# Two output stores split into 120 and 8 rows, so that fifteen and eight DMA engines carry them instead of sixteen

## The chip, the core and the metric

The kernel runs on one core of a Trainium2 chip. The core has computing engines that run side by side, each on its own list of instructions: TensorE (PE; its weight loads are shown as PEld), VectorE (DVE), ScalarE (ACT) and GpSimd (POOL). SyncE (SP) computes nothing here and issues transfers. Transfers between the chip's memory (HBM) and the on-chip memory (SBUF, 128 partitions) are carried by sixteen DMA engines. The results of TensorE land in PSUM and are copied from there to SBUF by VectorE or ScalarE before they can be stored.

The metric is the time of one execution on the device, in microseconds (us), taken without the profiler. The profile comes from an execution of its own, which is longer.

## What is computed

The reference takes 1,024 sequences of 50 item numbers, their lengths, and a table of 100,001 embeddings of 128 numbers. It gathers the embeddings, takes running means, normalises them, runs a spiking recurrence over the 50 steps, and multiplies the spike counts with the whole table. Cut to what matters:

```python
emb = emb_table.at[0].set(0.0)
e = emb[seq]                                   # 1024 x 50 x 128
uF = cumsum(e, axis=1) / minimum(t, lengths)
y = (uF - mean) * rsqrt(var + BN_EPS) * gamma + beta
# 50 steps: v = v + (x - v) / TAU ; spike = v >= V_TH ; v = v - spike * V_TH
uF_out = spikes.mean(axis=0)                   # 1024 x 128
scores = uF_out @ emb.T                        # 1024 x 100001, float32
```

The output has 1,024 x 100,001 x 4 bytes, 409.6 MB. The table is 51.2 MB.

## The kernel before

The first stage is the gather and the recurrence. The second stage, which the change touches, makes the product with the table. The table is worked through in 98 blocks of 1,024 rows (`HALF`), and these in 22 groups `c` of the widths below. For each group, the eight blocks `n` of 128 sequences follow one another. For each `n` an output tile `o` of 128 partitions is filled block by block: matmuls into PSUM (`product`), then a copy with the factor 1/50 into `o`, on VectorE and ScalarE in turn. Then one store sends the whole tile out.

```python
P = 128
HALF = 1024
KQ = HALF // P                                  # 8
WIDTHS = 4 * [2] + 4 * [3] + 11 * [6] + [4, 4, 4]
NARROW, MIDDLE = 4, 8
# ...
    def store(n, c0, o):
        nc.sync.dma_start(out=out[n * P : (n + 1) * P, c0 : c0 + o.shape[1]], in_=o)
```

From group 8 (`MIDDLE`) on, three tiles of six blocks take turns, so the tile of one store is filled again three stores later:

```python
                turns = [(rowp, "rows2", 6), (rowp, "rows3", 6), (op, "o", 6)]
# ...
        for n in range(NB):
            # ...
            pool, tag, most = turns[blocks % len(turns)]
            blocks += 1
            o = pool.tile([P, most * HALF], F32, tag=tag, name=f"o_{c}_{n}")
            for q in range(q0, q1):
                # ... matmuls of block q into po
                if turn % 2 == 0:
                    nc.vector.tensor_scalar_mul(o[:, h0 : h0 + hw], po[:, :hw], 1.0 / T)
                else:
                    nc.scalar.mul(o[:, h0 : h0 + hw], po[:, :hw], 1.0 / T)
                turn += 1
                # ...
            if c or n > 1:
                store(n, q0 * HALF, o[:, : min(N, q1 * HALF) - q0 * HALF])
            # ...
            if n in (1, 4) and c >= MIDDLE and to_fetch < parts:
                # ... ScalarE issues the load of three more blocks of the table
```

Below, store (c,n) is the one of group c and block n. A store of groups 8 to 18 has 128 rows of 6,144 numbers, 24,576 bytes a row. The last three groups have four blocks each, 16,384 bytes a row. The last block of the table has 673 rows; it is loaded in two small transfers, 128 x 5 rows and 33 rows of 512 bytes.

Of the kernel before, what the change touches and what calls it, by code (L numbers as in the profile page):

```python
# [20 lines left out]
P = 128  # L21
BN_EPS = 1e-5
V_TH = 1.0
HALF = 1024
KQ = HALF // P
# [4 lines left out]
HELD = AHEAD * GROUP + LATE  # L30

WIDTHS = 4 * [2] + 4 * [3] + 11 * [6] + [4, 4, 4]
NARROW, MIDDLE = 4, 8


@with_exitstack
def rec_kernel(
# [9 lines left out]
    nc = tc.nc  # L47
    B, T = seq.shape
    N, D = table.shape
# [24 lines left out]
    parts = -(-N // HALF)  # L74
    assert sum(WIDTHS) == parts
    rows = {}
# [6 lines left out]
    def size(q):  # L83
        return min(HALF, N - q * HALF)

    def slot(q):

        if q < GROUP + LATE:
            return 0, q % GROUP
        return (q - LATE) // GROUP, (q - LATE) % GROUP  # L90

    def group(g):
        at = g if g < AHEAD else AHEAD - 2 + g % 2
        r = rowp.tile([P, GROUP, HALF], F32, tag=f"rows{at}", name=f"rows_{g}")
        for k in range(GROUP):
            rows[g * GROUP + k + (LATE if g else 0)] = r[:, k, :]
        return r

    def fetch(r, q, n):

        engine = nc.sync if q < HELD else nc.scalar
        k = slot(q)[1]
        n = min(n, parts - q)
        whole = n - (size(q + n - 1) < HALF)
        if whole:
            engine.dma_start(
                out=r[:, k : k + whole, :],
                in_=table[q * HALF : (q + whole) * HALF, :].rearrange("(q p k) d -> p q (k d)", p=P, k=KQ),
            )
        if whole < n:  # L110
            full, rest = divmod(size(parts - 1), P)
            c1 = (parts - 1) * HALF
            r = r[:, k + whole, :].rearrange("p (k d) -> p k d", d=D)
            if full:
                engine.dma_start(
                    out=r[:, :full, :],
                    in_=table[c1 : c1 + full * P, :].rearrange("(k p) d -> p k d", p=P),
                )
            if rest:
                engine.dma_start(out=r[:rest, full, :], in_=table[c1 + full * P : N, :])  # L120
# [21 lines left out]
    def prepare(q, pt):  # L142
        turned(q, pt)
        split[q] = hi, lo = free.pop(0)
        hw = size(q)
        if hw % 2:
            nc.vector.memset(hi[:, hw : hw + 1].bitcast(F32), 0.0)
            nc.vector.memset(lo[:, hw : hw + 1].bitcast(F32), 0.0)
        vp, vh, vl = views(q, pt, hi, lo)
        nc.scalar.copy(vh, vp)  # L150
        nc.vector.tensor_tensor(vl, vp, vh.bitcast(F32), ALU.subtract)  # L151
# [3 lines left out]
    def product(po, q, n, k0, kw):  # L155
        kw += kw % 2
        for j, part in enumerate(split[q]):
            nc.tensor.matmul(  # L158
                po[:, :kw],
                lhsT=counts[n],  # L160
                rhs=part[:, k0 : k0 + kw],
                start=j == 0,
                stop=j == 1,
            )

    def store(n, c0, o):
        nc.sync.dma_start(out=out[n * P : (n + 1) * P, c0 : c0 + o.shape[1]], in_=o)


    with ExitStack() as ph:  # L170
# [132 lines left out]
        for t in range(T):  # L303
# [10 lines left out]
            pieces = halves if not last else halves[:1] + [slice(B - 3 * P, B), slice(BANK, BANK + P)]  # L314
# [102 lines left out]
        for q, (pool, tag, po) in enumerate(((gp, "e", sums), (up, "uF", [po1[:, cs] for cs in halves]))):  # L417
            o = pool.tile([P, HALF], F32, tag=tag, name=f"o_0_{q}")
            for h, cs in enumerate(halves):
                product(po[h], q, 0, h * BANK, BANK)  # L420
            for h, cs in enumerate(halves):
                if q and h:
                    nc.vector.tensor_scalar_mul(o[:, cs], po[h], 1.0 / T)
                else:
                    nc.scalar.mul(o[:, cs], po[h], 1.0 / T)
                store(0, q * HALF + h * BANK, o[:, cs])
# [10 lines left out]
    q0 = 0  # L437
    to_split = WIDTHS[0]
    to_fetch = HELD

    def places(at):
        t = rowp.tile([P, GROUP, HALF], F32R, tag=f"rows{at}", name=f"pairs_{at}")
        free.extend((t[:, k, :], t[:, k + 1, :]) for k in range(0, GROUP, 2))

    for c, W in enumerate(WIDTHS):

        if c in (0, NARROW, MIDDLE):
            opening.close()
            where = opening if c < MIDDLE else ctx
            op = where.enter_context(tc.tile_pool(name="o", bufs=1, reuse_waits="tile"))  # L450
            if c == 0:
                third = [op.tile([P, HALF], F32R, tag=x, name=x) for x in ("hi2", "lo2")]
                free.append(third)
                turns = [(op, f"o{k}", 2) for k in range(4)]
            elif c == NARROW:
                assert third in free
                free.remove(third)
                turns = [(op, f"o{k}", 3) for k in (2, 0, 1)]
            else:
                fourth = op.tile([P, 4, HALF], F32R, tag="pairs", name="pairs")  # L460
                free.extend((fourth[:, k, :], fourth[:, k + 1, :]) for k in (0, 2))
                turns = [(rowp, "rows2", 6), (rowp, "rows3", 6), (op, "o", 6)]
            blocks = 0
        q1 = q0 + W
        q2 = q1 + (WIDTHS[c + 1] if c + 1 < len(WIDTHS) else 0)

        def ready():
            nonlocal to_split
            if to_split < q2 and free:
                prepare(to_split, psum.tile([P, HALF], F32, tag="ps", name=f"pt_{to_split}"))  # L470
                to_split += 1

                if to_split in (GROUP + LATE, 2 * GROUP + LATE):
                    places(to_split // GROUP - 1)

        for n in range(NB):
            if c == 0 and n == 0:
                continue
# [4 lines that stand above are left out]
                h0 = (q - q0) * HALF  # L483
                hw = size(q)
                po = psum.tile([P, HALF], F32, tag="ps", name=f"po_{n}_{q}")
                for k0 in range(0, hw, BANK):
                    product(po[:, k0 : k0 + BANK], q, n, k0, min(BANK, hw - k0))
# [5 lines that stand above are left out]
                if c == 0 and n == 1:  # L493
                    store(n, q * HALF, o[:, h0 : h0 + hw])
                if n == NB - 1:
                    free.append(split.pop(q))
                    ready()
            if c or n > 1:
                store(n, q0 * HALF, o[:, : min(N, q1 * HALF) - q0 * HALF])
            if 2 <= n < NB - 1:  # L500
                ready()

            if n in (1, 4) and c >= MIDDLE and to_fetch < parts:
                g, k = slot(to_fetch)
                if k or to_split >= (g - 1) * GROUP + LATE:
                    if k == 0:
                        r = group(g)
                    fetch(r, to_fetch, GROUP // 2)
                    to_fetch += GROUP // 2
        assert to_split == q2  # L510
        q0 = q1
# [19 lines left out]
```

## Time and profile before

| | |
|---|---|
| time of one execution, median of 3 | 1574.13 us (1574.05 to 1574.31) |
| the profiled execution | 1643.7 us from the first to the last instruction |
| written to HBM, read from HBM | 409.6 MB, 77.7 MB |
| busy in the span: PE, PEld, DVE, ACT, POOL | 67%, 50%, 58%, 38%, 23% |
| copies PSUM to `o`: VectorE, ScalarE | 391 of 1221 ns each, 391 of 1018 ns each |
| stores of 3,072 KB (six blocks) | 88 |
| loads of 1,536 KB during the second stage | 19 |
| one issue of a store on SyncE | 332 ns |

The page of a profile has six parts: busy times; the span in forty slices, with a digit for the busy share of each engine and of the sixteen DMA engines together; the DMA queues; the chain of work that ended last; the costliest groups of instructions; and the issues of transfers. In the chain, each step is followed back to what released it: "DMA scores<-o" there is the time from the issue of a store to its landing. A line of the waits such as "ACT o L491 <- DMA scores<-o" means that line 491 on ScalarE, which writes a tile `o`, waited for the store of that tile's earlier contents; the numbers after it are the total in us, how often, and the longest.

A store has landed when all the DMA engines that carry it have reported. The trace has these reports one by one, sixteen for a whole store, and a record for each row that was moved, with its start, size and duration.

### The profile page before, as it was taken

The page shows a single profiled execution, that of the slowest core. Times are in us where ns is not written, and L with a number is a line of the kernel's source. Part 1 is how long each engine was busy: PE and PEld are TensorE (multiplying, and loading weights), DVE is VectorE, ACT ScalarE, POOL GpSimd, SP SyncE. Part 2 cuts the span into 40 slices and gives each one's busy share as a digit, 9 for nine tenths or more (in the row PEclk, how much of TensorE's full clock was granted, in tenths as well). Part 3 has the DMA queues.
Part 4 walks back from the last instruction along what each step waited for, and adds up shares of the span by engine and source line. Part 5 has one row for each costly group of instructions (what it writes and reads, how often), then busy time and mean ns, then how long its engine had stood idle before and what let it go on. Part 6 is the DMA issues. An engine that isn't in the chain of part 4 may idle for free.

```text
span 1643.7 us, 12618 instructions
## 1 busy us (share of the span) xinstructions
PE 1108.6 (67%) x4548; PEld 825.2 (50%) x4548; DVE 945.6 (58%) x1165; ACT 630.2 (38%) x700; POOL 378.3 (23%) x406
## 2 busy tenths in 40 slices
PE   4334334344343499888988888878788887887885
PEld 2122122122122276666866666666666666665664
DVE  4566566566575766566655555555545554554553
ACT  2222222222222255455544444444444444443442
POOL 7666666666666500000000000000000000000000
PEclk9975555555555599999999999999999999998998
DMA  9511111111112179999999999999999999999998
GB/s 340 216 46 48 47 46 49 47 45 48 49 45 70 39 319 416 403 422 417 400 427 431 429 429 424 423 424 423 426 427 415 416 419 429 427 408 415 391 424 361
DMA packets 54859, 488.14 MB, mean 297 GB/s; under 512 B 12139, under 2 KB 12940, under 8 KB 32524
## 3 DMA queue, kind: packets, MB, share of 16 engines
q1 hardware_dynamic: 33424, 429.81, 62.3%
q0 software_dynamic: 12800, 26.24, 6.1%
q10 hardware_dynamic: 8572, 31.28, 4.8%
q8 instruction: 36, 0.59, 0.1%
q14 instruction: 27, 0.22, 0.0%
HBM read 77.69 MB, written 409.60 MB: 296 GB/s over the span
## 4 chain that ended last, share of the span: by engine, by line
DMA 47%; DVE 23%; another core or an unknown queue 11%; PE 9%; ACT 6%; issue 3%; DVEq 0%; POOL 0%; ACTq 0%; SPq 0%; POOLq 0%
DMA scores<-o 46%; PE po L158 9%; DVE bs L340 4%; ACT o L491 4%; DVE uF L332 4%; DVE v L377 4%; DVE s L360 3%; DVE negv L295 3%; DVE o L489 2%; DVE a L370 1%; DMA e<-in_L_rec_emb_table,idx 1%; DVE mv L348 1%; DVE q L367 1%; ACT v L374 0%
## 5 line engine op out<-in xcount | busy, mean ns | idle before, releaser
L489 DVE TENSOR_SCALAR o<-po 128x1024 f32<-128x1024 f32 x391 | 464.2, 1221 | 357.5 <-DMA scores<-o 304.1
L491 ACT ACTIVATE o<-po 128x1024 f32<-128x1024 f32 (+1 forms) x391 | 387.6, 1018 | 550.8 <-DMA scores<-o 331.1
L201 POOL DMA_INDIRECT e<-in_L_rec_emb_table,idx x400 | 377.7, 944 | 184.2 <-issue 112.8
L158 PE MATMUL po<-pairs,countB 128*128 128x512 f32 x1136 | 304.2, 414 | 65.9 <-ACT o L491 50.8
L158 PEld LDWEIGHTS po<-pairs,countB 128*128 128x128 f32 x1136 | 218.4, 197 | 129.0 <-ACT o L491 65.7
L158 PE MATMUL po<-pairs,countC 128*128 128x512 f32 x852 | 232.4, 419 | 49.4 <-ACT o L491 49.3
L267 PE MATMUL pre<-zT,l 128*128 128x512 f32 x100 | 74.4, 746 | 251.3 <-DVE uF L332 203.5
L158 PEld LDWEIGHTS po<-pairs,countC 128*128 128x128 f32 x852 | 164.5, 199 | 94.9 <-ACT o L491 61.0
L267 PEld LDWEIGHTS pre<-zT,l 128*128 128x128 f32 x100 | 27.7, 278 | 291.3 <-issue 175.0
L332 DVE SCALAR_TENSOR_TENSOR uF<-rlen,pre 128x512 f32<-128x512 f32 (+1 forms) x101 | 68.1, 674 | 167.5 <-remote 154.8
L352 ACT ACTIVATE r<-mv,eps 128x1 f32<-128x1 f32 x50 | 14.7, 295 | 364.6 <-DVE mv L348 297.8
L151 DVE TENSOR_TENSOR pairs<-pt,pairs 128x1024 fp32r<-128x1024 f32 x71 | 86.3, 1222 | 88.5 <-ACT pairs L150 88.3
L128 PE MATMUL pt<-ident,rows 128*128 128x128 f32 x782 | 110.1, 287 | 9.6 <-ACT o L491 5.7
L128 PEld LDWEIGHTS pt<-ident,rows 128*128 128x128 f32 x782 | 98.7, 150 | 30.8 <-ACT o L491 9.8
L323 PE MATMUL pre<-ident,e 128*128 128x128 f32 x400 | 102.1, 423 | 15.9 <-DMA e<-in_L_rec_emb_table,idx 13.8
L323 PEld LDWEIGHTS pre<-ident,e 128*128 128x128 f32 x400 | 85.7, 224 | 47.7 <-DMA e<-in_L_rec_emb_table,idx 23.9
L278 PE MATMUL sums<-s,ident_h 128*128 128x512 bf16 x98 | 49.6, 609 | 75.4 <-DVE s L360 44.3
L158 PE MATMUL po<-hi,countB 128*128 128x512 f32 x216 | 89.0, 412 | 16.3 <-ACT o L491 11.4
L158 PE MATMUL po<-lo,countB 128*128 128x512 f32 x216 | 86.2, 401 | 0.0
L150 ACT CAST pairs<-pt 128x1024 fp32r<-128x1024 f32 x71 | 71.8, 1012 | 13.7 <-PE pt L128 13.4
L158 PE MATMUL po<-hi,countC 128*128 128x512 f32 (+1 forms) x162 | 67.9, 419 | 13.6 <-ACT o L491 13.6
L158 PE MATMUL po<-pairs,countA 128*128 128x512 f32 x284 | 71.3, 395 | 8.1 <-ACT o L491 8.0
(75 smaller groups left out, 876.4 us busy)
## 6 DMA issues: line engine op xcount, KB each, us to landing
scores<-o SPq DMA_DIRECT2D x88, 3072.0 KB
scores<-o SPq DMA_DIRECT2D x32, 1536.0 KB
scores<-o SPq DMA_DIRECT2D x16, 2048.0 KB
scores<-o SPq DMA_DIRECT2D x30, 1024.0 KB
rows<-in_L_rec_emb_table ACTq DMA_DIRECT2D x19, 1536.0 KB
rows<-in_L_rec_emb_table SPq DMA_DIRECT2D x6, 3072.0 KB
scores<-o SPq DMA_DIRECT2D x8, 1872.5 KB
e<-in_L_rec_emb_table,idx POOLq DMA_INDIRECT x400
```

The costliest lines, as they stand in the source:

```text
L128: nc.tensor.transpose(pt[:, k0 : k0 + kw], r[:kw, k0 : k0 + D], ident[:kw, :kw])
L150: nc.scalar.copy(vh, vp)
L151: nc.vector.tensor_tensor(vl, vp, vh.bitcast(F32), ALU.subtract)
L158: nc.tensor.matmul(po[:, :kw], lhsT=counts[n], rhs=part[:, k0 : k0 + kw], start=j == 0, stop=j == 1,)
L201: nc.gpsimd.indirect_dma_start(out=es[t][:, n * P : (n + 1) * P], out_offset=None, in_=table, in_offset=bass.IndirectOffsetOnAxis(ap=idx[: ...
L267: nc.tensor.matmul(pre[h], lhsT=l, rhs=zT[:, h * BANK : (h + 1) * BANK], start=t == 0, stop=False, skip_group_check=True,)
L323: nc.tensor.matmul(pre[h][:, k : k + P], lhsT=e[:, c0 : c0 + P], rhs=ident, start=False, stop=last, is_transpose=True, skip_group_check=True,)
L332: nc.vector.scalar_tensor_tensor(uF[:, cs], rlen[:, cs], 1.0 / (t + 1), pre[h][:, cs.start - h * BANK : cs.stop - h * BANK], ALU.max, ALU. ...
L340: nc.vector.bn_stats(bs[:, j, :], uF[:, cs])
L377: nc.vector.scalar_tensor_tensor(vt, negv[:, cs], -0.5, vt, ALU.mult, ALU.add)
L489: nc.vector.tensor_scalar_mul(o[:, h0 : h0 + hw], po[:, :hw], 1.0 / T)
L491: nc.scalar.mul(o[:, h0 : h0 + hw], po[:, :hw], 1.0 / T)
```

## The change

At two of the stores, (10,4) and (16,4), the tile goes out in two pieces: rows 0 to 119, then rows 120 to 127. A store of 128 rows is divided among sixteen DMA engines, eight rows each. The change is meant to divide 120 rows among fifteen, again eight rows each, and the 8 rows among eight, one row each, so that the sixteenth engine has no part in these two stores and can catch up with others. Nothing else changes.

```diff
 WIDTHS = 4 * [2] + 4 * [3] + 11 * [6] + [4, 4, 4]
+RELIEF = {(10, 4), (16, 4)}
 NARROW, MIDDLE = 4, 8

-    def store(n, c0, o):
-        nc.sync.dma_start(out=out[n * P : (n + 1) * P, c0 : c0 + o.shape[1]], in_=o)
+    def store(n, c0, o, pieces=(P,)):
+        b = 0
+        for m in pieces:
+            nc.sync.dma_start(out=out[n * P + b : n * P + b + m, c0 : c0 + o.shape[1]], in_=o[b : b + m, :])
+            b += m

             if c or n > 1:
-                store(n, q0 * HALF, o[:, : min(N, q1 * HALF) - q0 * HALF])
+                pieces = (P - KQ, KQ) if (c, n) in RELIEF else (P,)
+                store(n, q0 * HALF, o[:, : min(N, q1 * HALF) - q0 * HALF], pieces)
```

## The prediction

> **What bounds the kernel now.** I read the forty slices first. The rows say when the transfers fill the time: the first third of the span is the recurrence (DMA digit 1), and from about 590 us on every digit is 9 and the last row stands near 425 GB/s.
>
> ```profile
> span 1643.7 us, 12618 instructions
> ...
> DMA  9511111111112179999999999999999999999998
> GB/s 340 216 46 48 47 46 49 47 45 48 49 45 70 39 319 416 403 422 417 400 427 431 429 429 424 423 424 423 426 427 415 416 419 429 427 408 415 391 424 361
> ```
>
> Then the table of stretches over the second stage. The columns after the length are busy time (and count) of PE, weight load, VectorE, ScalarE and GpSimd, then clock, DMA share, GB/s. No computing engine fills its 200 us; the DMA share is one. But it is not the same everywhere: it falls from 427 to 414 GB/s over the last three rows, though the stores there have the same rows of 24 KB.
>
> ```profile
> 800.00:1000.00 200.00, 168.43 (x756) 133.18 (x755) 110.83 (x94) 93.39 (x95) 0.00 (x0) 0.96 1.01 427
> 1000.00:1200.00 200.00, 161.77 (x704) 127.24 (x703) 105.12 (x89) 87.00 (x89) 0.00 (x0) 0.94 1.00 425
> 1200.00:1400.00 200.00, 165.29 (x718) 130.07 (x717) 104.47 (x90) 87.10 (x89) 0.00 (x0) 0.93 1.00 420
> 1400.00:1600.00 200.00, 166.81 (x717) 129.63 (x716) 106.28 (x92) 87.54 (x90) 0.00 (x0) 0.93 0.98 414
> ```
>
> The waits and the chain of work that ended last say how the stores hold up the rest: both engines that fill the output tiles wait for a tile whose store has not landed, and the chain goes store, a few matmuls, store.
>
> ```profile
> ACT o L491 <- DMA scores<-o: 331.1, 136, 5.7
> DVE o L489 <- DMA scores<-o: 304.1, 136, 5.4
> ```
>
> ```profile
> 1278.30 21.73 DMA scores<-o
> ...
> 1301.21 10.98 PE po L158 x40
> ...
> 1313.26 19.03 DMA scores<-o
> ```
>
> Last, the trace's DMA records themselves (one per row moved: start, size, duration; no engine's number) and the sixteen completions of each store. The 24 KB rows take 912 ns in the median, and 16 x 24,576 B / 912 ns = 431 GB/s: the engines run at their own rate. Laid end to end the rows form sixteen series with no gap to speak of. One series is slower: between 650 and 850 us the median of its 24 KB rows is 945 ns, against 916 to 919 in the fifteen others. Its effect shows in each store: how long the sixteenth completion comes after the middle one. That lag is 1.5 us at store (8,0), 5.5 us at (10,4), 8.1 us at (13,4), 6.2 us at (16,4), 5.5 us at (19,0), then 2.6 us at (19,2) after a pause that all share, and 5.0 us at the last store (landed 1642.7 us, the middle completion 1637.8). So one DMA engine is behind nearly all the time, and the stage waits for it where the three output tiles run out.
>
> [...] The trace agrees that one is (945 against 916 ns) and cannot say which, since its records carry no number; that the change picks the sixteenth is the hint that it is engine 15. [...] The sixteen completions per whole store agree for 128; nothing in this trace shows 120 or 8. [...] No line here shows two engines on one port; it is the ground of my second rival.
>
> **The change part by part.** Instructions of all computing engines keep their order; SyncE gets two more issues. At a store of six blocks (6,144 columns, 24 KB a row) each engine normally moves 8 rows, 8 x 0.912 = 7.3 us.
> - Removed: the sixteenth engine's share of two stores, 16 rows x about 0.94 us = 15.0 us of its work.
> - Added: [...] 2 x 0.912 = 1.8 us more for those eight. Two issues on SyncE at 332 ns each; it mostly waits for the tiles, so nothing on the path.
> - Moved: nothing else. A tile is now free when two transfers have landed.
>
> What is the slow engine's lag worth? Not its 15 us, since the others idle only where the lag exhausts the tiles. The gaps in the series, averaged over the sixteen, are 0.3 us from 850 to 1200, 0.2 from 1200 to 1300, 2.5 from 1300 to 1480: 3.0 us. From 1480 to 1540 they are 3.3 us, but there the stores (19,2) and (19,3) go out at 1531.5 and 1533.4, just when the last small loads of the table land (1531.4 and 1533.3, 41 to 43 short rows that take turns with the long ones); the relief does not remove that. It does resynchronise the engines. After it, the lag of the last store is 5.0 us; the next slowest series ends some 3.2 us before it, by the completions (1639.6).
>
> With the relief: at (10,4) the lag of 5.5 us becomes 5.5 - 7.5 = -2.0; it grows again by about (8.1 - 5.5) / (1165 - 963) = 0.013 us per us, so over the 400 us to (16,4) to about +3; the second relief sets it near -4. It never reaches the 6 to 8 us at which the others idle. So the 3.0 us go, and the slow engine enters the pause at 1530 level instead of 5.5 us behind; over the last 100 us it then loses 5.0 - 2.6 = 2.4 us again and ends 2.4 us behind the middle, about where the second slowest is, instead of 5.0: 2.6 us. Sum: -3.0 - 2.6 = -5.6[...]: **-3.8 us**. That is in the profiled execution (1643.7 us); I carry it over unscaled to the timed 1574.13, since the second stage is the same work: **1570 us**.
>
> **The rivals.** First, the lag is worth more: the compute that refills a tile starts at the sixteenth completion, so a lag of 6 us less might bring the issues forward throughout, and the fall from 427 to 414 GB/s over the last 300 us (3% of 300 = 9 us) might all be lag. For it: the waits above; against: the series show hardly a gap before 1300, and the loads share the blame. It would make the time about 1563.
>
> Second, **two engines on one port**. [...] At worst the 120 rows take twice 7.3 us, and the 8 rows 4 x 0.91 = 3.6 us. [...] up to 7.3 + 3.6 = 10.9 us per relieved store on engines that have no slack, 21.8 in all, less the 5.6 gained: +16, about 1590. Half of it[...]: 1579. Against: nothing in this trace shows such a doubling for stores, and the split may be dealt otherwise. I give it a third.
>
> Third, the slow engine is an artefact of the profiled execution, and the timed one has even engines. Then the change only adds 1.8 us: 1576.
>
> **Range and chances.** The first sum and the first rival together get over half, the port rival a third, the rest for no effect. The middle stays at 1570; the low end 1562 is the first rival with a little to spare, the high end 1586 leaves out only the full doubling. Two per cent would be 31 us: more than the 15 us of work removed and more than the 16 of the worst case. So within 2% gets 0.975, faster 0.01, slower 0.015.
>
> **What would show it.** Right: the sixteenth completion of the stores after (10,4) comes no later than the second slowest, the lag restarts below 1 us and stays under 5; the stretch 1200 to 1600 moves 420 GB/s or more; the lag at the last store is about 2.5 us; a few us between 1300 and 1480 gone. Port rival: the 24 KB rows of the two 120-row pieces last about 1.8 us instead of 0.91 and the eight short-piece rows longer still, with a dip in GB/s at these two stores. Wrong altogether: the latest engine of the stores after the relieved ones is as far behind as before, which would mean that the slow engine is not the sixteenth[...].

## The result and the profile after

| | before | after |
|---|---|---|
| time of one execution, median of 4 | 1574.22 us (1574.05 to 1574.47) | 1600.49 us (1598.9 to 1600.95) |
| ratio | | 1.0165 (95% interval 1.0147 to 1.0183) |
| the profiled execution | 1643.7 us | 1599.1 us |

The change costs 26.3 us. That is within 2%, but outside the predicted range of 1562 to 1586 us, and on the other side of the kernel before than the predicted 1570.

The two profiled executions differ by more than the change: in the first stage the granted TensorE clock was 0.98 in the one after and 0.61 in the one before, and that stage is some 71 us shorter. The lines are the stretches of the first stage (columns as in the prediction), after and before:

```profile
0.00:490.00 490.00, 246.79 (x609) 118.60 (x610) 351.20 (x639) 142.55 (x198) 368.30 (x395) 0.98 0.29 94
```

```profile
0.00:560.00 560.00, 216.95 (x616) 128.50 (x616) 351.85 (x640) 144.13 (x200) 375.82 (x404) 0.61 0.28 83
```

So the second stages are laid over each other by their stores: from (8,0) to (10,2) each store lands 71.2 us earlier after than before, to within 0.2 us. What follows counts from there.

The slices after have two dips in the last row, which the prediction's row of before does not have: 319 in slice 23, and 364 and 345 in slices 33 and 34.

```profile
span 1599.1 us, 12622 instructions
...
DMA  9611111111122999999999899999999998999898
GB/s 340 238 53 53 53 53 52 53 53 53 53 79 104 408 402 421 421 389 431 423 431 422 319 419 411 430 413 431 422 414 427 409 364 345 420 422 423 377 426 354
```

The stretches after, cut at the two changed stores, which were issued at 871.3 and 1289.2 us:

```profile
730.00:860.00 130.00, 111.98 (x498) 88.77 (x496) 74.48 (x64) 61.48 (x62) 0.00 (x0) 0.95 1.00 426
860.00:925.00 65.00, 44.92 (x192) 35.77 (x191) 28.02 (x24) 23.91 (x24) 0.00 (x0) 0.84 0.92 356
925.00:1275.00 350.00, 288.25 (x1243) 227.28 (x1241) 182.69 (x155) 152.59 (x155) 0.00 (x0) 0.93 1.00 420
1275.00:1345.00 70.00, 51.06 (x209) 40.04 (x208) 30.39 (x26) 25.21 (x26) 0.00 (x0) 0.83 0.90 344
1345.00:1480.00 135.00, 105.98 (x448) 82.96 (x448) 66.33 (x56) 54.91 (x56) 0.00 (x0) 0.92 1.01 422
```

The kernel before has, in about the same stretches of its own execution, 1.00 at 425 GB/s and 1.01 at 428:

```profile
930.00:995.00 65.00, 55.46 (x240) 43.32 (x238) 33.75 (x29) 27.77 (x29) 0.00 (x0) 0.93 1.00 425
1345.00:1415.00 70.00, 58.97 (x256) 46.51 (x255) 36.09 (x31) 31.39 (x32) 0.00 (x0) 0.92 1.01 428
```

The loss is in the second and the fourth line after. The DMA share falls to 0.92 and 0.90 there, the rate by twice as much, to 356 and 344 GB/s. So about half of the loss is idle time, while tiles wait for a late store, and half is engines that are busy and slow. A loss of 64 to 78 GB/s over 65 to 70 us is some 10 to 13 us at full rate.

The chain of work after, around store (10,4), and the longest waits. Before, the links of the chain from store to store are mostly 19 to 22 us. Here two follow one another of 26 and 27 us, the stores (10,3) and (10,6), and the link of the second piece of (16,4) has 32.5. The longest waits for a store are 12.9 us on VectorE and 9.7 on ScalarE, where they were 5.4 and 5.7.

```profile
837.71 19.39 DMA scores<-o
...
861.48 25.82 DMA scores<-o
...
893.24 27.29 DMA scores<-o
...
924.91 21.19 DMA scores<-o
...
1289.59 32.47 DMA scores<-o
```

```profile
ACT o L496 <- DMA scores<-o: 353.9, 135, 9.7
DVE o L494 <- DMA scores<-o: 326.9, 130, 12.9
```

The sixteen completions of each store tell it exactly. The table has the last completion of a store, after against before, with the 71.2 us taken out:

| store | last completion, us later than before | middle one |
|---|---|---|
| (10,2) | 0.0 | 0.0 |
| (10,3), whole, ahead of the split one | 4.2 | 0.0 |
| (10,4), 120 rows | 11.1 | 4.9 |
| (10,4), its 8 rows: 1.6 us behind the 120; then (10,5) | 12.8 | 6.7 |
| (11,0) to (16,2) | 12.3 to 13.3 | 10 to 13 |
| (16,3) | 18.7 | 13.1 |
| (16,4), 120 rows | 24.9 | 16.9 |
| (16,7) to the last store | 25.7 to 27.0 | 25 to 28 |
| the last store | 26.3 | 26.1 |

Each split costs 13 us, nothing is lost or won anywhere else, and the sum is the timed difference. The engine whose completion comes last (below: the late engine) was not relieved: at the last store its lag behind the middle is 5.1 us, as it was before (5.0).

Below, a 24 KB row is called stretched when it took over 1.1 us, where the median is 0.912. In the second stage 170 rows were stretched before, and 382 after: 212 more, where the two split stores have 256 rows. Of the 438 long rows that began between 870 and 905 us, 106 were stretched; they took 1.66 us in the median and 3.7 at the longest. From 850 to 870 us none of 299 was.

### The profile page after: what moved, and what is told of

Same layout as the page of the kernel before. It is cut to its first block, busy times and chain, and to the rows that moved or that the text cites. A ratio compares the mean times of both kernels' runs of the same rounds, so it can differ in the third digit from the quotient of the medians.

```text
span 1599.1 us, 12622 instructions
## 1 busy us (share of the span) xinstructions
PE 1149.0 (72%) x4548; PEld 824.0 (52%) x4548; DVE 947.4 (59%) x1165; ACT 630.8 (39%) x700; POOL 379.0 (24%) x406
## 4 chain that ended last, share of the span: by engine, by line
DMA 56%; POOL 17%; PE 10%; issue 8%; ACT 5%; DVE 3%; another core or an unknown queue 0%; DVEq 0%; POOLq 0%; ACTq 0%; SPq 0%
DMA scores<-o 47%; POOL e L206 17%; PE po L159 9%; DMA e<-in_L_rec_emb_table,idx 6%; ACT o L496 4%; DVE o L494 2%; DMA rows<-in_L_rec_emb_table 2%; ACT pairs L151 0%; PE pre L328 0%; PE pt L129 0%; DVE pairs L152 0%; DVE s L365 0%; DMA idx<-in_r_seq 0%; PE sums L283 0%; DVE bs L345 0%
## 5 line engine op out<-in xcount | busy, mean ns | idle before, releaser
L159 PE MATMUL po<-pairs,countB 128*128 128x512 f32 x1136 | 308.3, 418 | 65.7 <-ACT o L496 50.9
L328 PE MATMUL pre<-ident,e 128*128 128x128 f32 x400 | 147.8, 449 | 147.4 <-DMA e<-in_L_rec_emb_table,idx 147.4
L328 PEld LDWEIGHTS pre<-ident,e 128*128 128x128 f32 x400 | 79.1, 200 | 235.5 <-DMA e<-in_L_rec_emb_table,idx 211.4
L159 PE MATMUL po<-hi,countB 128*128 128x512 f32 x216 | 89.9, 416 | 15.7 <-ACT o L496 12.9
L151 ACT CAST pairs<-pt 128x1024 fp32r<-128x1024 f32 x71 | 71.8, 1011 | 13.5 <-PE pt L129 13.3
L379 ACT ACTIVATE v<-uF,hgb,a 128x1024 f32<-128x1024 f32 x49 | 59.2, 1208 | 42.2 <-DVE a L375 42.1
L159 PE MATMUL po<-pairs,countA 128*128 128x512 f32 x284 | 71.2, 396 | 4.6 <-ACT o L496 4.6
```

Source lines behind the costliest of these rows:

```text
L159: nc.tensor.matmul(po[:, :kw], lhsT=counts[n], rhs=part[:, k0 : k0 + kw], start=j == 0, stop=j == 1,)
L328: nc.tensor.matmul(pre[h][:, k : k + P], lhsT=e[:, c0 : c0 + P], rhs=ident, start=False, stop=last, is_transpose=True, skip_group_check=True,)
L379: nc.scalar.activation(vt, uF[:, cs], AF.Identity, bias=hgb[:, 1:2], scale=a)
```

## The experiments

The **port theory** is the prediction's second rival, an assumption of the author's: at a store that is not a whole one, two DMA engines get in each other's way on the SBUF side, as if at one port, and a row takes twice its time or more. No record shows a port. Where an expectation counts the engines ("the first seven", "the sixteenth"), that is assumed too, as no record carries an engine's number. The theory's rivals: the second transfer, or the fifteen engines, cost by themselves; rows collide on the HBM side; or the loads do it. Beside them stood the question which engine is late. The diffs are cut to what matters. The runs were on chips whose first stages differ, on which the kernel before takes 1573.88 to 1649.53 us; a ratio is always to the kernel before on the same chip.

**Only the 120 rows.** The short piece is left out, so 8 rows of the output are not written at two stores.

```diff
-                pieces = (P - KQ, KQ) if (c, n) in RELIEF else (P,)
+                pieces = (P - KQ,) if (c, n) in RELIEF else (P,)
```

> The two stores send rows 0 to 119 alone; rows 120 to 127 of their two blocks are left unwritten. Port theory[...]: the 120-row piece keeps its stretched rows of about 1.8 us, only the 8-row piece's share goes, about 4 us a store: near 1590. Second-transfer theory (what costs is that a store is two transfers, the 120 rows are fine): near 1572.

Measured: 1667.59 us against 1646.39, ratio 1.0140 (1.0111 to 1.0168), 21 us. The 120-row piece alone carries nearly all of the cost, with one transfer to a store. The second-transfer theory falls. The late engine's time from (10,3) to (10,4) is 15.7 us here, as in the changed kernel, where the pieces of 8 rows then add 1.6 us; the port theory's figure of 4 for them was too high. The longest row after the first split took 3.7 us here too, so the rows far above 1.8 us are not those of the short piece; what makes them so long is not shown. In the stretches the two dips are there as in the changed kernel:

```profile
930.00:995.00 65.00, 47.56 (x197) 37.59 (x196) 29.41 (x25) 24.24 (x25) 0.00 (x0) 0.84 0.93 362
995.00:1345.00 350.00, 287.44 (x1244) 225.92 (x1242) 182.81 (x155) 152.74 (x156) 0.00 (x0) 0.93 1.00 420
1345.00:1415.00 70.00, 51.09 (x209) 40.27 (x208) 31.22 (x27) 26.28 (x28) 0.00 (x0) 0.85 0.90 345
```

**Two halves.** No engine is meant to be left out of either piece.

```diff
-                pieces = (P - KQ, KQ) if (c, n) in RELIEF else (P,)
+                pieces = (P // 2, P // 2) if (c, n) in RELIEF else (P,)
```

> The same two stores go out as 64 and 64 rows, so both pieces run on all sixteen engines, four rows each, and nobody is relieved. Port theory: [...] all rows of these stores last about 1.8 us, 7.3 us more a store and a drain behind it: 1588 to 1600. Theory that fifteen engines, an odd share, or the short piece is the cause: 64 rows divide by 16, so 1574 to 1576. Theory of conflicts on the HBM side: [...] 1574 to 1576.

Measured: 1655.33 us against 1646.39, ratio 1.0065 (1.0042 to 1.0088). The cost of 9 us is below the port theory's 14 to 26, but it is clear, and both rivals had none. 327 rows are stretched, 157 more than before, where the two stores have 256; why not all of them are stays open. The middle completions of (10,3), the first half and the second lie at 950.1, 957.3 and 965.0 us: 14.9 us for eight rows an engine, about twice 7.3. The stretch around the store, first in this kernel, then at the same store in the kernel before:

```profile
955.00:975.00 20.00, 12.18 (x46) 9.47 (x45) 8.20 (x7) 5.93 (x7) 0.00 (x0) 0.75 0.99 348
```

```profile
946.00:966.00 20.00, 15.62 (x71) 12.45 (x72) 10.64 (x10) 9.37 (x10) 0.00 (x0) 0.91 1.00 428
```

The DMA share, the mean of sixteen engines, is 0.99 and 1.00; the rates are 348 and 428 GB/s. So no engine need be left out for the loss.

**One split store.**

```diff
-RELIEF = {(10, 4), (16, 4)}
+RELIEF = {(10, 4)}
```

> Only store (10,4) is split into 120 and 8 rows. If each split costs by itself: half of the 26 us, near 1587. If the first split costs and the second only finds the stage disturbed, or the reverse: near 1574 or near 1600.

Measured: 1656.71 us against 1646.39, ratio 1.0072 (1.0050 to 1.0095): 10 us, half within the interval. The splits cost each by itself; the second dip is gone from the stretches.

```profile
930.00:995.00 65.00, 44.46 (x191) 35.02 (x190) 28.96 (x25) 24.55 (x25) 0.00 (x0) 0.84 0.93 362
995.00:1345.00 350.00, 287.45 (x1246) 226.80 (x1245) 183.05 (x156) 153.07 (x156) 0.00 (x0) 0.93 1.00 420
1345.00:1415.00 70.00, 56.91 (x251) 44.36 (x250) 37.50 (x33) 30.87 (x32) 0.00 (x0) 0.95 1.00 425
```

**A split store where no loads run.**

```diff
-RELIEF = {(10, 4), (16, 4)}
+RELIEF = {(20, 4)}
```

> Only store (20,4) is split, in the last groups, where rows have 16 KB (615 ns) and no loads run. Port theory: rows of the 120-row piece near 1.23 us, of the 8-row piece up to 2.5 us, 5 to 7 us in all, near 1580. Theory that the collision is with the loads of the table: rows stay at 615 ns, and the relief of 8 x 0.63 = 5 us of the late engine shows instead, 1570 to 1573. If the late engine is the sixteenth, its lag at the last store is near zero or gone.

Measured: 1650.22 us against 1646.39, ratio 1.0032 (1.0017 to 1.0047), 3.8 us. In the trace, from the last completion of (20,3) to that of the last store it takes 62.1 us, where the kernel before takes 56.9: 5.2 us. Six other runs that leave these stores whole take 56.5 to 56.9 there. No load runs there (in the trace before, the last one lands at 1533.3 us and (20,3) at 1585.8), so the loads have no part in it. Of the 172 rows that began between 1583 and 1594 us, 91 took over 1.0 us; 1.2 to 1.27 us is common, twice the usual 0.61, and the longest take 3.0 to 4.0. In the stretches of this kernel and, at the same stores, of the kernel before, the rate falls from 423 to 255 GB/s at a full DMA share:

```profile
1578.00:1583.00 5.00, 4.66 (x26) 3.67 (x25) 3.49 (x4) 2.87 (x4) 0.00 (x0) 1.00 1.01 423
1583.00:1593.00 10.00, 8.36 (x37) 6.10 (x35) 4.12 (x6) 3.12 (x4) 0.00 (x0) 1.00 1.03 255
```

```profile
1574.00:1584.00 10.00, 9.35 (x46) 7.16 (x46) 7.45 (x9) 5.62 (x6) 0.00 (x0) 1.00 1.04 441
```

Here the engine that was left out can be seen: in the next store one completion comes at 1594.0 us, 4.5 us ahead of the middle one. And the last completion keeps falling behind the one ahead of it by 0.12 to 0.14 us a store (0.63, 0.76, 0.88, 1.02 us), the late engine's own pace, as in the kernel before. The engine left out is one, the late engine another.

**Every ninth row.** If rows collide by where they lie in SBUF, the spacing of a piece's partitions must matter. The author assumed that partitions nine apart are free of it and partitions eight apart are not, and that pieces of 15 or 14 rows still leave an engine out; no run so far had shown either.

```diff
-    def store(n, c0, o):
-        nc.sync.dma_start(out=out[n * P : (n + 1) * P, c0 : c0 + o.shape[1]], in_=o)
+    def store(n, c0, o, step=1):
+        for i in range(step):
+            nc.sync.dma_start(out=out[n * P + i : (n + 1) * P : step, c0 : c0 + o.shape[1]], in_=o[i:P:step, :])
 # ...
+                step = 9 if (c, n) in RELIEF else 1
```

> Both stores go out as nine pieces of every ninth row: two of 15 rows and seven of 14[...]. Port theory: no row is stretched, the pieces take about nine rows per engine (8.2 us instead of 7.3) and 0.33 us an issue; the cost falls from 13 us a store to 1 to 3, so within 6 us of the kernel before. If the late engine is among the first eight, no gain: its lag does not fall. If it were the sixteenth: 4 us faster. Theory that fewer than sixteen engines or several transfers for a store cost by themselves: as slow as the changed kernel, 20 us or more.

Measured: 1658.73 us against 1649.53, ratio 1.0060 (1.0036 to 1.0083), 9 us where at most 6 were expected. The stretched rows are gone: 156, fewer than the 170 of the kernel before. The time is lost otherwise. SyncE waits with the seventh piece of (10,4), from 953.9 to 964.5 us, for a load of the table to land, and meanwhile the engines run dry; at (16,4) it waits 10.9 us in the same way. The lines are SyncE's wait and the stretch in which it falls:

```profile
SPq L170 <- DMA rows<-in_L_rec_emb_table: 10.7, 1, 10.7
```

```profile
930.00:955.00 25.00, 20.54 (x93) 16.04 (x91) 12.62 (x12) 10.35 (x11) 0.00 (x0) 0.93 0.99 401
955.00:968.00 13.00, 7.11 (x32) 5.75 (x32) 3.14 (x3) 3.52 (x4) 0.00 (x0) 0.77 0.42 165
```

Transfers take turns on eight semaphores in this program (numbers 100 to 105, 117 and 118 in the second stage of the trace before), and nine pieces in a row come round to that of a load still under way. The DMA share of 0.42 tells this loss from the other kind, which has a share near one (0.99 around the halves, 1.03 at (20,4)).

**Every eighth row.** The control: eight pieces of 16 rows, with partitions eight apart.

```diff
-                step = 9 if (c, n) in RELIEF else 1
+                step = 8 if (c, n) in RELIEF else 1
```

> The same two stores in eight pieces of every eighth row, sixteen rows each[...]. Port theory: all rows stretched to about 1.8 us, 7 us more a store, 10 to 20 us in all, clearly slower than the pieces of every ninth row. Theory of the number of pieces or of engines: as those of every ninth row, or faster[...].

Measured: 1666.24 us against 1649.53, ratio 1.0105 (1.0086 to 1.0123). It has the same wait for a load (10.6 us) and one piece less, and is 7.5 us slower than every ninth row; 145 rows take over 1.5 us, against 44. This difference goes with the spacing of the rows; as rows eight partitions apart also lie eight rows apart in HBM, the last two runs below are needed to tell the two sides apart.

**Every ninth row where no loads run.** The edit is that of every ninth row, with store (20,4).

> Store (20,4) alone in nine pieces of every ninth row, where no loads run. Port theory: rows stay at about 615 ns, where the split into 120 and 8 rows had 1.2 us. Late engine: if it is among the first fourteen, its lag grows by 0.12 us a store as before and the pieces' last completion is the late engine's; if it is the fifteenth or sixteenth, the last completions of the next stores are level with the others.

Measured in one execution: 1644.19 us, beside 1649.53 (1645.24 to 1650.94) for the kernel before, too few to call it faster. In the trace, from the last completion of (20,3) to that of the last store it takes 58.9 us, against 56.9 before and 62.1 with 120 and 8 rows. The rows have a median of 618 ns, and seven of 326 exceed 1.0 us. The pieces of 15 and of 14 rows each have a straggler, a last completion that is 2.7 us behind the one ahead of it at first: the late engine takes part in them all. In the first seven pieces these last completions follow one another at 0.62 to 0.66 us, while in the first four the ones ahead of them do at 0.60 to 0.63.

**Which engine is late: pieces of seven rows.**

```diff
+        for i in range(step):
+            rows_ = range(i, P, step)
+            cuts = (0, len(rows_)) if step == 1 else (0, 7, len(rows_))
+            for a, b in zip(cuts, cuts[1:]):
+                lo, hi = rows_[a], rows_[b - 1] + 1
 # ... a store of the rows lo, lo + step, ... below hi
```

> Store (20,4) alone in eighteen pieces of every ninth row: sixteen of 7 rows[...] and two of 8 rows[...]. If the late engine is the eighth: the pieces of 7 rows land within a few tenths of us of one another and only those of 8 rows have a straggler, and behind the store the late engine has lost 8 x 0.63 us of work and is level with the engines that have nothing to do. If it is one of the first seven: every piece has a straggler, and it is still the last by 2 us or more afterwards.

Measured in one execution: 1655.51 us. Each of the first seven-row pieces has its last completion 2.0 to 2.1 us behind the one ahead of it, so the late engine takes part in pieces of seven rows too. The second half of that expectation did not hold: behind the store the late engine was only 0.0 us last, as the pieces went out at 0.8 us each and the other engines waited for them.

**Which engine is late: pieces of one to fourteen rows.**

```diff
+        cuts = {0: (0, 1, 3, 7, 15), 1: (0, 3, 8, 15), 2: (0, 6, 14)}
 # ... as before, with these cuts for i = 0, 1, 2 and none for the others
```

> Store (20,4) in pieces of every ninth row, of 1, 2, 4, 8, 3, 5, 7, 6, 8 and six times 14 rows, to find the number of the late engine: [...] Every piece of seven rows had one, so a straggler is due from m = 7 on at the latest[...].

Measured in one execution: 1578.16 us, beside 1573.88. At store (20,3) the middle completion is at 1509.7 us, the second last at 1511.6, the last at 1514.3. If each engine takes its rows in the order of issue, which is an assumption, no piece that lands before 1514.3 has a row of the late engine. Then:

| rows, in order | last completion | what it says |
|---|---|---|
| 1 | 1510.4 | level with the middle: not in it |
| 2 | 1511.1 | before 1514.3: not in it |
| 4 | 1512.7 | before 1514.3: not in it |
| 8 | 1514.9 | 1514.3 + 0.63: the late engine's row |
| 3 | 1513.7 | earlier than the piece ahead of it: not in it |
| 5 | 1515.6 | 1514.9 + 0.63: its next row |
| 7, then 6 | 1516.2, 1516.8 | its next two |

So on this chip the late engine had no part in the pieces of one to four rows, and a part in those of five to eight. The number of completions agrees in each piece, m rows and one more; which engines a piece runs on, and so the late engine's number, no record shows. Of the pieces sent here, those that spared it had four rows at most.

**HBM or SBUF.** Two kernels that move 112 rows in eight pieces of 14 at (20,4), with the steps on the two sides exchanged. Sixteen partitions stay unsent and rows land in one another's places.

The first is shown; in the second, 8 and 9 change places.

```diff
+        for i in range(8):
+            nc.sync.dma_start(
+                out=out[n * P + i : n * P + i + 13 * 8 + 1 : 8, c0 : c0 + o.shape[1]],
+                in_=o[i : i + 13 * 9 + 1 : 9, :],
+            )
```

> At store (20,4) eight pieces of 14 rows read partitions nine apart and write HBM rows eight apart; sixteen partitions stay unsent and the rows land permuted. Port theory: nothing is stretched, rows at 615 ns. Theory that rows eight apart collide in HBM: rows near 1.2 us.

> The reverse: eight pieces of 14 rows read partitions eight apart and write HBM rows nine apart[...]; sixteen partitions stay unsent, rows permuted. Port theory: [...] most of the 112 rows last about 1.2 us. Theory of HBM: rows at 615 ns.

Measured in one execution each, 1574.89 and 1575.84 us. The rows counted are those that began in some 17 us around the pieces, rows of the neighbouring stores among them. With eight apart in HBM, they have a median of 616 ns and five of 335 exceed 1.0 us. With eight apart in SBUF, 75 of 277 do, where 112 are in question. Rows nine apart in HBM were not stretched in the run with every ninth row either. The collision is on the SBUF side. The stretches of the two, first eight apart in HBM, then in SBUF:

```profile
1506.00:1516.00 10.00, 9.31 (x44) 7.05 (x42) 6.56 (x9) 5.37 (x7) 0.00 (x0) 1.00 0.80 322
```

```profile
1506.00:1517.00 11.00, 10.22 (x48) 7.75 (x46) 7.24 (x9) 5.62 (x6) 0.00 (x0) 1.00 0.80 257
```

The DMA share is 0.80 in both; the same share moves 322 and 257 GB/s.

## Why the prediction was wrong, step by step

- **What bounds the kernel** held: sixteen engines busy throughout, one of them late, output tiles waiting for its completion. The completions after show it more sharply than the prediction had it: in this trace the end follows the late engine alone. What that engine lost, the end lost (4.2 + 6.9 + 1.7 us at (10,4), 13 us to the end).
- **"the hint that it is engine 15"** failed first. The late engine took part in every piece of 15, 14, 8, 7 and 5 rows. In the one run that had such pieces, it took no part in those of one to four rows; its number no record shows. The trace of the kernel before had a sign that was passed over: the load of the table's last 33 rows has twelve completions, where a whole store has sixteen, and its last comes 6.1 us behind the one ahead of it (1533.3 after 1527.2 us). Its completions are spread too widely, from 1511 us on, to prove it, but a straggler there speaks for a late engine that such a transfer does not leave out.
- **"Removed: ... 15.0 us of its work"** and the -5.6 us from it were therefore 0. The lag did not restart below 1 us; it rose to 11.7 us at (10,4), and stood at 5.1 instead of 2.4 at the end, which was the prediction's own sign that the slow engine is not the sixteenth. What a relief of the right engine would bring was not tried, as no such split was found.
- **"2 x 0.912 = 1.8 us more for those eight"**, the step from -5.6 to -3.8 us, counted rows at 912 ns. The rows of the relieved stores were stretched instead, to about twice that (1.66 us in the median of the 106), and this was the **second rival**. Of the 30 us between the predicted 1570 and the measured 1600, this is the larger part: 26.3 us where 1.8 were added, beside the 5.6 that never came. Of the rival's mechanism the experiments show this much: with partitions eight apart 75 of 277 rows exceeded 1.0 us, with as many pieces and rows nine apart 5 of 335. That two engines meet at one port is not shown. Its sum was mis-sized, from factors that were assumed and that no trace showed: two for the 120 rows, four for the eight. The worst case was put at 10.9 us a store, measured are 13: 4.2 us while the late engine is still at the store ahead (the term that was missed; what slows it there is not shown), 6.9 for the 120 rows (7.3 was put) and 1.7 for the eight (3.6 was put). And 5.6 us were subtracted that never came: 1574.2 + 26.3, not 1590.
- **"Moved: nothing else"** held, as did the small cost of two issues: the second piece of (10,4) went out 0.5 us behind the first.
- **The first rival** (the lag is worth more) was not tested, since the lag was never reduced. **The third** (even engines without the profiler) was not tested either: the loss is the same in the trace and in the timed executions, 26.2 and 26.3 us, but no run tells the late engine's pace in an execution without the profiler.
- **The chances.** A third for the port rival was too little. What spoke against it was that nothing in the old trace showed such a doubling, and that was misread. Of the 11,264 rows of 24 KB there, 55 took over 1.5 us, fourteen of them 1.811 us, twice 0.906, and 54 of the 55 while rows of a load were being moved. What stretched these is not shown, but a row of a store that takes double its time was there to see. The whole stores, whose rows take 912 ns, do not speak against it: the old trace has no store of 120 rows.

How 120 rows are dealt among the engines is not shown; the records do not name rows or engines. Measured is the stretched rows' median of 1.66 us, 1.8 times 912 ns. Why the late engine is slower by about three per cent (from (20,0) to (20,7) before, a store took 5.07 us by its last completion and 4.93 by its middle one) stays open, as does whether it is the same one on every chip.

## What to carry to other kernels

Before relieving a late DMA engine, find out whether the transfer that is meant to spare it does: a straggler among its completions, here 2.0 to 2.7 us behind the one ahead, says that the late engine takes part, and the trace at hand may have such a transfer already, as the load of 33 rows here. Look also at how long each row of a store of another shape takes: of the 438 rows around the first split, 106 took 1.66 us in the median instead of 0.912, and with partitions eight apart rows were stretched as well, with partitions nine apart not (75 of 277 and 5 of 335 over 1.0 us). The mark of this was a rate that fell further than the DMA share (255 GB/s at 1.03, 356 at 0.92), while a wait in the issue showed as a low share (165 GB/s at 0.42). Here, where tiles wait for the last of sixteen completions, what the late engine lost was lost to the end: 12.8 us at (10,4), and 12.3 to 13.3 at the stores from (11,0) to (16,2).

## What the hardware showed besides

- A row of 24 KB took 912 ns in the whole stores; the 106 stretched rows at the first split took 1.66 us in the median, and single ones up to 3.7. For rows of 16 KB the figures are 0.61 us, 1.2 to 1.27 and up to 4.0.
- A transfer of fewer than sixteen rows had one completion more than rows, the first 0.4 to 3.2 us after its issue: the 8-row pieces have nine reports, those of seven rows eight. The 120 rows have sixteen, the first 0.5 us after the issue at (20,4).
- The store ahead of a split one was hurt as well: (10,3) by 4.2 us at the late engine and not at all at the middle one.
